# One of the seven products of an attention kernel's last V projection, moved from the projection into the third-last step

## The chip, the cores and the metric

The kernel runs on one core of one Trainium2 chip. The metric is the device time of one execution in microseconds, the median of several; less is better.

## The reference

`x` has 8 batches of 512 tokens with 512 features; there are 16 heads of 32. Of each batch:

```python
Q, K, V = heads(x @ Wq.T + bq), heads(x @ Wk.T + bk), heads(x @ Wv.T + bv)
cQ = Q + heads(cond @ Wq.T + bq)      # one condition token per batch
cK = K + heads(cond @ Wk.T + bk)
attn = softmax(cQ @ cK.T / sqrt(32))  # per head, 512 x 512
out = x + merge(attn @ V)
```

All inputs, outputs and the large matmuls are float32.

## The kernel before

**Steps.** The work is cut into T = 32 steps: step t is one batch b = t // 4 and one group g = t % 4 of four heads (128 columns of the output). The last batch, b = 7, is steps 28 to 31. Each step has four quarters (in the last steps called rows), one for each block of 128 keys. In quarter i of step t the program issues, in this order:

- `exponentials(t, i)`: four short matmuls (L560) that put the negated row maxima into four PSUM banks, four matmuls (L563) that add the scores, with the keys along the partitions, and four exponentials on ACT (L574) from PSUM to SBUF.
- `row_max(t + 1, i + 1)` (of step t + 2 in the last quarter): four score matmuls for the next step (L499), each into a bank of its own, and their maxima on DVE (L490 for one bank, L508 for two). Up to step 29 ACT then also runs `denominators` on them (L518, each followed by a read of its accumulator).
- one more piece of PE work: a part of the next batch's projections, or `weighted`, the exponentials times V (L579) with the sum of the denominators (L610).

The engines' orders are written out by hand (a manual schedule), so each engine issues its instructions in the order of the program, and semaphores are set where data or a bank demands it.

**Banks.** All eight PSUM banks are one tile. `banks(i)` is the i-th bank of the present line of the table `TURNS`: entries 0 to 3 go to the exponentials, 4 to 7 to the row maxima. The quarter's extra work reuses entries 0 to 3 after ACT has read them. `advance()` goes to the next line; in the last three steps `row(i)` sets it to `TURNS[8 + i]`:

```python
(4, 5, 6, 7, 0, 1, 2, 3),   # row 0
(6, 7, 0, 1, 2, 3, 4, 5),   # row 1
(0, 1, 2, 3, 4, 5, 6, 7),   # row 2
(2, 3, 4, 5, 6, 7, 0, 1),   # row 3
```

**Projections.** Q, K and V of a batch are made with Strassen's scheme in Winograd's form: seven products of half-size blocks (L403 for V, L406 for Q and K), each of two matmuls of 128 x 256 (two records each in the trace), for each half u = 0, 1. `first_products` does products 1, 6, one of the two matmuls of product 2, and 7; `other_products` does 4, 5, the rest of 2, and 3. So each call has seven matmuls. ACT copies product 1 to SBUF (L438) and DVE adds the others up: L444, L445 and L426 (in `plus`) after the first, L458, L459 and L426 after the others. In between `small()` calls `transpose_max` (L544 on PE, L550 on DVE), which prepares the next step's maxima.

V lies in `vs[b % 2]` as [128, 4, 512]: four blocks of 128 tokens and 512 features. `parts_of` names its parts for half u: c1 and c12 in the left 256 columns (heads of groups 0 and 1), c2 and c22 in the right 256 (groups 2 and 3). Product 7 goes only into the right half.

Batch 7's projections are made in steps 25 to 28: Q in the first quarter, K in the third, V in the fourth, by `project_pair`. Steps 25 and 27 call the `first` form, 26 and 28 the `other`. V's left half is first read in step 29, its right half in step 30 (`part_of(t, banks(0), [0])` with t = 30).

**The last three steps** (29, 30, 31) have no projections left. Their extra work is `part_of`: times V for single key blocks, copied out by ACT (L775, L769) and added by POOL (L770); `masked` and `spread_sums` for the denominators (POOL L600, PE L610). From step 30 on the program for DVE also adds exponentials up (L845, L847), and the end is a chain of DVE, PE and ACT.

Of the kernel before, what the change touches and what calls it, by code (L numbers as in the profile page):

```python
# [12 lines left out]
ALU = mybir.AluOpType  # L13
# [4 lines left out]
def kernel(  # L18
# [38 lines left out]
    nc = tc.nc  # L57
    P = 128
    B, S, D = x.shape
# [9 lines left out]
    HS = S // 2  # L69
# [41 lines left out]
    def banks(i, n=1):  # L111

        j = TURNS[turn[0]][i]
        if n == 1:
            return psum[:, j, :]
        k = TURNS[turn[0]][i + 1]
        return psum[:, j : k + 1 : k - j, :]
# [127 lines left out]
    for i in range(NS):  # L245
        r = slice(i * BL, (i + 1) * BL)
# [95 lines left out]
    def pair_of(t, n):  # L342

        if (n, t // 2) not in pairs:
            pairs[n, t // 2] = qkp.tile([P, 2, S], F32, tag=n, name=f"{n}T_{t // 2}")
        return pairs[n, t // 2]
# [30 lines left out]
    def block_of_w(n, i, u, kc):  # L377
        f = MADE_OF[i - 1][0]
        if n == "v":
            at = slice(0, HS) if f != "22" else slice(HS, D)  # L380
            if isinstance(f, int):
                return wc[n][:, f, kc, :]
        else:
            g = u * 2 + (f == "22")
            at = slice(g * P, (g + 1) * P)
            if isinstance(f, int):
                return wc[n][:, f, kc, u * P : (u + 1) * P]
        return wT[n][:, kc + 2 * (f != "11"), at]

    def block_of_x(b, i, kc, at):  # L390
        f = MADE_OF[i - 1][1]
        if isinstance(f, int):
            return xc[:, f, kc, at]
        off = HS * (f == "22")
        return xT[b][:, kc + 2 * (f != "11"), at.start + off : at.stop + off]

    def product(n, b, u, i, pt, kcs=(0, 1)):

        for kc in kcs:
            w = block_of_w(n, i, u, kc)  # L400
            if n == "v":
                xb = block_of_x(b, i, kc, slice(u * P, (u + 1) * P))
                nc.tensor.matmul(pt, xb, w, start=(kc == kcs[0]), stop=(kc == kcs[-1]))  # L403
            else:
                xb = block_of_x(b, i, kc, slice(0, HS))
                nc.tensor.matmul(pt, w, xb, start=(kc == kcs[0]), stop=(kc == kcs[-1]))  # L406

    def twice(a):
        return a.unsqueeze(1).broadcast_to([P, 2, HS])

    def halves(a):
        return a.rearrange("p (h s) -> p h s", h=2)


    def parts_of(n, b, u):

        if n == "v":
            v = vs[b % 2]
            return v[:, u::2, :HS], v[:, u + 2, :HS], v[:, u::2, HS:], v[:, u + 2, HS:]
        o = pair_of(b * G + u * 2, n)  # L420
        return halves(o[:, 0, :]), o[:, 0, HS:], halves(o[:, 1, :]), o[:, 1, HS:]
# [26 lines left out]
    def other_products(n, b, u, dens, small, at):  # L448
# [12 lines left out]
        if n != "v":  # L461
            for g in range(2):
                qkT[n, b * G + u * 2 + g] = pair_of(b * G + u * 2, n)[:, g, :]

    def project_pair(n, b, r, dens, small, at):

        if b >= B:
            dens()
            small()
        else:  # L470
            (first_products, other_products)[r % 2](n, b, r // 2, dens, small, at)


    nmax = {}
# [7 lines left out]
    def row_max(t, qc):  # L482
        if t >= T:
            return
        open_max(t)
        for j in range(HG):
            row_scores(t, qc, j, banks(HG + j))
        if t < T - 2 or t * NS + qc == T * NS - 1:
            for j in range(2):
                nc.vector.tensor_reduce(  # L490
                    nmax[t][:, qc, j : j + 1, 0], banks(HG + j), AX.X, ALU.max, negate=True
                )
        else:
            row_max_of(t, qc, 0, banks(HG, 2))
        row_max_of(t, qc, 1, banks(HG + 2, 2))
# [16 lines left out]
    def denominators(t, qc, prs=range(NP)):  # L512

        if t >= T - 2:
            return
        for j in [pr * 2 + i for pr in prs for i in range(2)]:
            dead = op.tile([P, S], F32, tag="dead", name=f"dead_{t}_{qc}_{j}")
            nc.scalar.activation(  # L518
                dead,
                banks(HG + j),  # L520
                AF.Exp,
                bias=nmax[t][:, qc, j, :],
                accum_out=sums[t][:, qc, j, :],
            )
# [14 lines left out]
    def transpose_max(t, bank, copy=nc.vector.tensor_copy):  # L539
        if t >= T:  # L540
            return
        pt = bank.bitcast(BF16)
        for qc in range(NS):
            nc.tensor.transpose(  # L544
                pt[:, qc * P : (qc + 1) * P],
                split[t % 2][:, qc, :, :].rearrange("p h e -> p (h e)"),
                identb,
            )
        maxT[t] = op.tile([P, S], BF16, tag="maxT", name=f"maxT_{t}")
        copy(maxT[t], pt[:, :S])  # L550
# [4 lines left out]
    def exponentials(t, kc, at=None):  # L555

        bank = [psum[:, i, :] for i in at] if at else [banks(i) for i in range(HG)]
        for j in range(HG):
            r = slice(j * HD, j * HD + 3)
            nc.tensor.matmul(bank[j], onesb[r, :], maxT[t][r, :], start=True, stop=False)  # L560
        for j in range(HG):
            r = slice(j * HD, (j + 1) * HD)
            nc.tensor.matmul(  # L563
                bank[j],
                qkT["k", t][r, kc * P : (kc + 1) * P],
                qkT["q", t][r, :],
                start=False,
                stop=True,
            )
        for pr in range(NP):  # L570
            e = ep.tile([P, 2, S], F32, tag="e", name=f"e_{t}_{kc}_{pr}")
            es[t, kc, pr] = e
            for i in range(2):
                nc.scalar.activation(e[:, i, :], bank[pr * 2 + i], AF.Exp)  # L574

    def times_v(t, kc, pt, chunks=range(NS)):
        b, g = divmod(t, G)
        for j in range(HG):
            nc.tensor.matmul(  # L579
                pt[j * HD : (j + 1) * HD, :],  # L580
                vs[b % 2][:, kc, (g * HG + j) * HD : (g * HG + j + 1) * HD],
                es[t, kc, j // 2][:, j % 2, :],
                start=(kc == chunks[0]),
                stop=(kc == chunks[-1]),
            )
# [11 lines left out]
    def masked(t):  # L597

        apart = op.tile([P, HG, NS, NS], F32, tag="apart", name=f"apart_{t}")
        nc.gpsimd.tensor_tensor(  # L600
            apart,
            sums[t].rearrange("p c h o -> p h c o").broadcast_to([P, HG, NS, NS]),
            which.unsqueeze(1).unsqueeze(1).broadcast_to([P, HG, NS, NS]),
            ALU.mult,
        )
        return apart

    def spread_sums(apart, pd):
        for h in range(HG):
            nc.tensor.matmul(  # L610
                pd[h * BL : (h + 1) * BL, :NB],
                modulo,
                apart[:, h].rearrange("p c a -> p (c a)"),
                start=True,
                stop=True,
            )
# [144 lines left out]
    def part_of(t, pt, of, between=None):  # L761

        for k, kc in enumerate(of):
            if k and between:
                between()
            times_v(t, kc, pt, of)
        if t in parts:
            p = op.tile([P, S], F32, tag="dead", name=f"part_{t}_{of[0]}")
            nc.scalar.copy(p, pt)  # L769
            nc.gpsimd.tensor_tensor(parts[t], parts[t], p, ALU.add)  # L770
        else:
            if not parts:
                parts["all"] = stage.tile([P, NC, D], F32, tag="w", name="parts")
            parts[t] = parts["all"][:, t % NC, :]
            nc.scalar.copy(parts[t], pt)  # L775

    def denominators_of(t, pd):

        den = op.tile([P, NB, 1], F32, tag="den", name=f"den_{t}")
        nc.scalar.copy(den, pd[:, :NB].unsqueeze(2))  # L780
        return den
# [6 lines left out]
    for t in range(T - 3):  # L788
        b, r = divmod(t, G)
# [4 lines left out]
        dens = lambda: denominators(t + 1, 1)  # L794
# [11 lines left out]
        dens = lambda: denominators(t + 1, 2)  # L806
# [13 lines left out]
        dens = lambda: denominators(t + 1, 3)  # L820
# [11 lines left out]
        dens = lambda: denominators(t + 2, 0)  # L832

        def small():
            transpose_max(t + 1, banks(2 if r % 2 else 1))
# [17 lines left out]
    def row(i):  # L853
        turn[0] = 8 + i
# [9 lines left out]
    exponentials(t, 1)  # L864
    row_max(t + 1, 2)
    part_of(t - 1, banks(0), [2])
    apart = masked(t - 1)
    row(2)
    exponentials(t, 2)
# [2 lines left out]
    part_of(t - 1, banks(0), [3])  # L872
    spread_sums(apart, banks(1))
    den = denominators_of(t - 1, banks(1))
    row(3)
    exponentials(t, 3)
    row_max(t + 2, 0)
# [69 lines left out]
    b, g = divmod(t, G)  # L947
# [48 lines left out]
```

## Time and profile before

| | us |
|---|---|
| median of 3 runs (732.04 to 732.4) | 732.4 |
| profiled execution, whole | 734.05 |
| its span, first to last instruction | 732.3 |
| PE busy with matmuls | 722.3 |
| ACT busy | 617.7 |
| DVE busy | 535.7 |
| POOL busy | 177.0 |

The granted clock of TensorE was 0.997 of full speed over the span. Engine shares are of the span; a busy PE includes pipelined matmuls that overlap. "L499" is line 499 of the kernel before. Where the text gives starts of single instructions to a hundredth of a microsecond, they are the trace's records, counted from the span's start. "x8" of a float32 matmul group means records: each float32 matmul leaves two.

### The profile page before, as it was taken

The page shows a single profiled execution, that of the slowest core. Times are in us where ns is not written, and L with a number is a line of the kernel's source. Part 1 is how long each engine was busy: PE and PEld are TensorE (multiplying, and loading weights), DVE is VectorE, ACT ScalarE, POOL GpSimd, SP SyncE. Part 2 cuts the span into 40 slices and gives each one's busy share as a digit, 9 for nine tenths or more (in the row PEclk, how much of TensorE's full clock was granted, in tenths as well). Part 3 has the DMA queues.
Part 4 walks back from the last instruction along what each step waited for, and adds up shares of the span by engine and source line. Part 5 has one row for each costly group of instructions (what it writes and reads, how often), then busy time and mean ns, then how long its engine had stood idle before and what let it go on. Part 6 is the DMA issues. An engine that isn't in the chain of part 4 may idle for free.

```text
span 732.3 us, 15085 instructions
## 1 busy us (share of the span) xinstructions
PE 722.3 (99%) x5396; PEld 401.8 (55%) x5396; DVE 535.7 (73%) x857; ACT 617.7 (84%) x1540; POOL 177.0 (24%) x276
## 2 busy tenths in 40 slices
PE   8999999999999999999999999999999999999996
PEld 5466555566555566555566555566555566555431
DVE  4698767777768777678676777677677777667676
ACT  2489988989898898898899898898898899898664
POOL 3622221122221122221122221122221122221351
PEclk9999999999999999999999999999999999999998
DMA  7734221222221222221222221222110111110121
GB/s 185 118 49 72 45 39 22 43 35 40 45 36 27 42 35 39 45 44 21 38 40 35 44 41 27 37 40 34 30 30 11 21 30 30 30 30 13 18 30 30
DMA packets 208111, 29.64 MB, mean 40 GB/s; under 512 B 205722, under 2 KB 206746, under 8 KB 208036
## 3 DMA queue, kind: packets, MB, share of 16 engines
q1 hardware_dynamic: 207184, 27.88, 23.7%
q8 instruction: 42, 0.69, 0.4%
q10 hardware_dynamic: 852, 0.81, 0.4%
q14 instruction: 33, 0.27, 0.1%
HBM read 20.27 MB, written 8.39 MB: 39 GB/s over the span
## 4 chain that ended last, share of the span: by engine, by line
PE 96%; DVE 2%; issue 1%; DMA 1%; SPq 0%; DVEq 0%
PE psum L406 26%; PE psum L499 16%; PE psum L579 15%; PE psum L563 14%; PE psum L403 14%; PE psum L560 6%; PE psum L350 2%; PE psum L544 1%; DMA x<-in_x_dram 1%; DVE acc L847 1%; PE psum L266 0%; DVE acc L845 0%; PE psum L657 0%; PE psum L589 0%; PE psum L610 0%
## 5 line engine op out<-in xcount | busy, mean ns | idle before, releaser
L518 ACT ACTIVATE dead<-psum,nmax 128x512 f32<-128x512 f32 x480 | 327.5, 702 | 5.3 <-DVE nmax L490 3.0
L574 ACT ACTIVATE e<-psum 128x512 f32<-128x512 f32 x512 | 264.3, 602 | 75.5 <-PE psum L563 75.4
L490 DVE TENSOR_REDUCE nmax<-psum 128x1 f32<-128x512 f32 x242 | 155.8, 685 | 143.3 <-PE psum L499 143.3
L508 DVE TENSOR_REDUCE nmax<-psum 128x2 f32<-128x1024 f32 x135 | 163.3, 1214 | 9.6 <-PE psum L499 8.3
L636 POOL TENSOR_TENSOR res<-res,recs 128x512 f32<-128x512 f32 x31 | 32.5, 1048 | 454.7 <-DVE res L635 454.7
L499 PE MATMUL psum<-kT,qT 32*128 32x512 f32 x1024 | 136.4, 601 | 0.0
L563 PE MATMUL psum<-qT,kT 32*128 32x512 f32 x1024 | 132.4, 588 | 0.0
L579 PE MATMUL psum<-e,v 128*32 128x512 f32 x1024 | 121.2, 596 | 0.0
L518 ACT ACTIVATION_READ_ACCUMULATOR dead<-psum,nmax 128x1 f32 x480 | 105.0, 219 | 0.0
L499 PEld LDWEIGHTS psum<-kT,qT 32*128 32x128 f32 x1024 | 58.1, 183 | 56.2 <-ACT dead L518 23.1
L579 PEld LDWEIGHTS psum<-e,v 128*32 128x32 f32 x1024 | 26.7, 110 | 65.8 <-issue 38.4
L563 PEld LDWEIGHTS psum<-qT,kT 32*128 32x128 f32 x1024 | 51.0, 185 | 2.2
L560 PE MATMUL psum<-maxT,onesb 3*128 3x512 bf16 x512 | 51.7, 384 | 0.5 <-DVE maxT L550 0.5
L403 PE MATMUL psum<-wc_v,xc 128*128 128x256 f32 x192 | 49.3, 379 | 0.0
L560 PEld LDWEIGHTS <-onesb 3*128 3x128 bf16 x512 | 13.4, 91 | 61.1 <-issue 51.7
L406 PE MATMUL psum<-xc,wc_q 128*128 128x256 f32 x180 | 46.2, 379 | 0.0
L406 PE MATMUL psum<-xc,wc_k 128*128 128x256 f32 x180 | 46.2, 379 | 0.0
L174 POOL TENSOR_TENSOR xr<-xr,bvs 128x512 f32<-128x512 f32 x31 | 39.4, 1270 | 17.6 <-DMA xr<-in_x_dram 17.6
L637 POOL TENSOR_TENSOR res<-res,xr 128x512 f32<-128x512 f32 x31 | 39.5, 1273 | 2.4
L403 PEld LDWEIGHTS psum<-wc_v,xc 128*128 128x128 f32 x192 | 36.5, 190 | 5.0
L403 PE MATMUL psum<-wT_v,xT 128*128 128x256 f32 x128 | 38.7, 405 | 0.0
L406 PEld LDWEIGHTS psum<-xc,wc_q 128*128 128x128 f32 x180 | 34.2, 190 | 4.7
(157 smaller groups left out, 771.5 us busy)
## 6 DMA issues: line engine op xcount, KB each, us to landing
xr<-in_x_dram SPq DMA_DIRECT2D x124, 64.0 KB, 2.4
out_dram<-res SPq DMA_DIRECT2D x124, 64.0 KB, 2.0
x<-in_x_dram SPq DMA_DIRECT2D x112, 64.0 KB, 2.4
w_q<-in_L_cond_Wq_dram SPq DMA_DIRECT2D x4, 256.0 KB, 4.9
w_v<-in_L_cond_Wv_dram SPq DMA_DIRECT2D x16, 64.0 KB, 2.5
w_k<-in_L_cond_Wk_dram SPq DMA_DIRECT2D x16, 48.0 KB, 2.4
x<-in_x_dram SPq DMA_DIRECT2D x2, 256.0 KB
x<-in_x_dram ACTq DMA_DIRECT2D x2, 256.0 KB, 4.4
```

What stands on the lines that cost most here:

```text
L174: nc.gpsimd.tensor_tensor(xr[t], xr[t], bias, ALU.add)
L403: nc.tensor.matmul(pt, xb, w, start=(kc == kcs[0]), stop=(kc == kcs[-1]))
L406: nc.tensor.matmul(pt, w, xb, start=(kc == kcs[0]), stop=(kc == kcs[-1]))
L490: nc.vector.tensor_reduce(nmax[t][:, qc, j : j + 1, 0], banks(HG + j), AX.X, ALU.max, negate=True)
L499: nc.tensor.matmul(pt, qkT["q", t][r, qc * P : (qc + 1) * P], qkT["k", t][r, :], start=True, stop=True,)
L508: nc.vector.tensor_reduce(nmax[t][:, qc, pr * 2 : pr * 2 + 2, 0], pt, AX.X, ALU.max, negate=True)
L518: nc.scalar.activation(dead, banks(HG + j), AF.Exp, bias=nmax[t][:, qc, j, :], accum_out=sums[t][:, qc, j, :],)
L560: nc.tensor.matmul(bank[j], onesb[r, :], maxT[t][r, :], start=True, stop=False)
L563: nc.tensor.matmul(bank[j], qkT["k", t][r, kc * P : (kc + 1) * P], qkT["q", t][r, :], start=False, stop=True,)
L574: nc.scalar.activation(e[:, i, :], bank[pr * 2 + i], AF.Exp)
L579: nc.tensor.matmul(pt[j * HD : (j + 1) * HD, :], vs[b % 2][:, kc, (g * HG + j) * HD : (g * HG + j + 1) * HD], es[t, kc, j // 2][:, j % 2, ...
L637: nc.gpsimd.tensor_tensor(y, y, xr.pop(t), ALU.add)
```

## The change

For V of the last batch, `project_pair` calls two new forms without product 7. The first does products 1, 6 and the whole of 2, the other 4, 5 and 3: six matmuls each instead of seven. DVE adds the parts up without product 7: still two additions after the first and three after the other, but c2 is added first, and c12 is updated twice after it. `add_m7(u, bank)` does product 7 later, two matmuls into a bank, and one addition of 128 x 2 x 256 on DVE into the right half of V. It is called in step 29: for u = 0 in row 1, after `part_of(t - 1, banks(0), [2])`, into `banks(1)` (bank 7); for u = 1 in row 2, after `denominators_of`, into `banks(2)` (bank 2). ACT, POOL and DMA instructions stay what they were.

```diff
+    def first_but_m7(n, b, u, dens, small, at):
+        one_, two_ = banks(0), banks(at)
+        c1, c12, c2, c22 = parts_of(n, b, u)
+        m1 = c2[:, 0, :]
+        product(n, b, u, 1, one_[:, :HS])
+        nc.scalar.copy(m1, one_[:, :HS])
+        dens()
+        product(n, b, u, 6, two_[:, :HS])
+        small()
+        product(n, b, u, 2, two_[:, HS:])
+        nc.vector.tensor_tensor(c12, two_[:, :HS], m1, ALU.add)
+        nc.vector.tensor_tensor(c1[:, 0, :], two_[:, HS:], m1, ALU.add)
+
+    def other_but_m7(n, b, u, dens, small, at):
+        dens()
+        one_, two_ = banks(at[0]), banks(at[1])
+        product(n, b, u, 4, one_[:, :HS])
+        product(n, b, u, 5, one_[:, HS:])
+        small()
+        product(n, b, u, 3, two_[:, :HS])
+        c1, c12, c2, c22 = parts_of(n, b, u)
+        nc.vector.tensor_tensor(c2, halves(one_), twice(c12), ALU.add)
+        nc.vector.tensor_tensor(c12, one_[:, HS:], c12, ALU.add)
+        nc.vector.tensor_tensor(c12, two_[:, :HS], c12, ALU.add)
+
+    def add_m7(u, pt):
+        c2 = parts_of("v", B - 1, u)[2]
+        product("v", B - 1, u, 7, pt[:, :HS])
+        nc.vector.tensor_tensor(c2, twice(pt[:, :HS]), c2, ALU.add)
+
     def project_pair(n, b, r, dens, small, at):
...
-            (first_products, other_products)[r % 2](n, b, r // 2, dens, small, at)
+            how = (first_products, other_products)
+            if n == "v" and b == B - 1:
+                how = (first_but_m7, other_but_m7)
+            how[r % 2](n, b, r // 2, dens, small, at)
...
     part_of(t - 1, banks(0), [2])
+    add_m7(0, banks(1))
     apart = masked(t - 1)
     row(2)
...
     den = denominators_of(t - 1, banks(1))
+    add_m7(1, banks(2))
     row(3)
     exponentials(t, 3)
```

## The prediction

> **What bounds the kernel now.** I read the page first (busy shares, then the chain that ended last), then the chain in order of time around the change, then the instructions of DVE and ACT beside it.
>
> ```profile
> span 732.3 us, 15085 instructions
> PE 722.3 (99%) x5396; PEld 401.8 (55%) x5396; DVE 535.7 (73%) x857; ACT 617.7 (84%) x1540; POOL 177.0 (24%) x276
> PE 96%; DVE 2%; issue 1%; DMA 1%; SPq 0%; DVEq 0%
> ```
>
> PE is the bound nearly everywhere, so 0.4 us of matmuls taken out of a PE-bound quarter can be worth 0.4 us, if ACT and DVE are ready that much sooner. The chain in order of time shows the quarter that loses a matmul (step 28, V) and the rows that gain the product (step 29):
>
> ```profile
> 678.67 1.92 PE psum L403 x8
> 680.59 0.22 PE psum L544 x4
> 680.81 1.35 PE psum L403 x6
> 682.16 0.33 PE psum L560 x4
> ...
> 689.11 0.72 PE psum L560 x4
> 689.82 0.86 PE psum L563 x8
> 690.68 1.02 PE psum L499 x8
> 691.70 0.99 PE psum L579 x8
> 692.70 0.05 PE psum L610 x7
> 692.75 0.66 PE psum L560 x4
> 693.40 0.86 PE psum L563 x8
> 694.26 1.02 PE psum L499 x8
> ```
>
> Columns: start, length, what. An L403 matmul is two records. L560 normally takes 0.33 and L499 0.86. In rows 2 and 3 of step 29 they take 0.72 and 1.02, then 0.66 and 1.02: 0.39 + 0.16 and 0.33 + 0.16 us of waiting, 1.04 in all, which extra matmuls could fill. DVE in the same rows:
>
> ```profile
> 688.15 2.36 DVE L508 TENSOR_REDUCE nmax<-psum 128x2 f32<-128x1024 f32 x2 [1.54 <-PE psum L499]
> 691.74 2.35 DVE L508 TENSOR_REDUCE nmax<-psum 128x2 f32<-128x1024 f32 x2 [1.23 <-PE psum L499]
> ```
>
> It reduces row 1's scores until 690.5 and row 2's until 694.1, and has 1.23 us free between. So its queue is far behind PE when PE enters row 3 at 692.75.
>
> **Part 1: a matmul less in each V quarter of steps 25 to 28.** Each quarter goes from 7 matmuls (14 records) to 6. Records of one run are 0.216 us apart, so PE needs 0.43 us less, four times: 1.72 us at most. DVE and ACT work there is the same in amount but does not start earlier, since it follows the scores at the quarter's head. So I ask when the next scores (L499 of the following row) find their banks free:
>
> ```profile
> 616.98 0.22 ACT L518 ACTIVATION_READ_ACCUMULATOR dead<-psum,nmax 128x1 f32 x1
> ...
> 638.98 0.20 ACT L518 ACTIVATION_READ_ACCUMULATOR dead<-psum,nmax 128x1 f32 x1
> ...
> 681.37 0.41 DVE L458 TENSOR_TENSOR v<-psum,v 128x256 f32<-128x256 f32 x1
> 681.70 0.68 DVE L459 TENSOR_TENSOR v<-psum,v 128x512 f32<-128x512 f32 x1
> 682.30 0.68 DVE L426 TENSOR_TENSOR v<-psum,v 128x512 f32<-128x512 f32 x1
> ```
>
> These are the last denominators of steps 25 and 26, and DVE's three additions of step 28. A release reaches PE about 0.05 us later (L508 ends at 690.51, L499 starts at 690.56).
> - Step 25: L499 started at 617.56 and could start at 617.13. The last denominator ends at 617.20 and holds one of its banks, so 617.25: 0.31 gained. Step 27 has the same spacing (661.35; denominator ends at 660.99): 0.31.
> - Step 28: L499 started at 683.18 and could at 682.75. The three additions are now in another order, 0.68, then 0.41, then 0.41, each waiting for the one before. From 681.37 they end at about 682.95 to 683.05, where L426 read its bank until 682.98 with nobody waiting. The fourth score uses that bank: start at about 683.03, 0.15 gained.
> - Step 26: L499 started at 639.40. Denominator until 639.18, additions from 637.60 until 639.2 to 639.3: about 0.10 gained.
>
> Sum: 0.87 us. The bounds are 0 and 1.72; I take the middle because each cover has a row. No DMA, SP or POOL instruction moves.
>
> **Part 2: the first product and addition, in row 1 of step 29.** Without a wait L560 would start at 689.04 (0.545 after the second half of L579, as at 685.45 to 686.00). The product's first record starts there, the second 0.32 later (656.76 to 657.08), two more at 0.216, then 0.31 to L560 (659.95 to 660.26). L560 starts at 690.10: four records cost 1.06 us, since the switches between tile shapes are paid once more. By then its banks are free and the 0.55 of waiting in row 2 is gone. Row 2 then runs clean: L563 at 690.33, L499 at 691.18, L579 at 692.15 (2.045 after L560, as 685.996 to 688.039) instead of 691.63. Row 2 is 0.51 us late. The first addition (0.68, by L459) lies in DVE's gap, 690.44 to 691.12, just before the fourth score needs bank 7 at 691.19. I price that new wait at nothing; if the addition is 0.2 us later, it is 0.2 us and a restart.
>
> **Part 3: the second product and addition, row 2.** This is where I expect the loss. The product goes to bank 2, which is the first bank of row 3's exponentials. In the changed program the first L560 of row 3 waits for DVE, where it waited for ACT. DVE is in order: the addition stands behind both reductions of row 2. L499's second half at 691.61, plus 0.63 (691.10 to 691.74), starts them at 692.24; the second starts 1.14 later, and the addition another 1.14 later, at 694.53. It ends at 695.2 and L560 starts at 695.26. The product itself is ready: after L610 (693.08) it starts at 693.2 to 693.4 and lands at 694.45 to 694.65, just about when DVE is free; so the addition may be up to 0.12 late. All of row 3 is queued behind that L560: L563, L499, ACT's exponentials and the next reductions. L579 of row 3 starts 2.045 later, at 697.3 to 697.4, instead of 695.22. That is 2.1 to 2.2 us late; with 0.1 for the restart (L499 took 1.14 instead of 1.03 after its wait at 690.56) I take 2.25. It contains Part 2's 0.51 and the used-up waits. After row 3 the chain runs PE, then DVE, without slack, until the end: nothing gives the time back. The POOL splits and the output DMAs shift with it.
>
> The nearest rows bound Part 3: if nobody waited for the addition, the rows would be 2.12 - 1.04 = 1.1 late; with a later addition and both restarts, 2.7.
>
> A page speaks on the addition's start: the Trainium skill, "VectorE: DVE Perf Modes", section "The DRAIN you can't avoid", says that the next op doesn't start until the pipe has emptied. The row differs: reductions recorded at 1.22 us start 1.14 apart. [...]
>
> The other is "TensorE: Matmul & The Clock Gate", section "Back-to-back issue gap": 262 cycles at 2.4 GHz, 0.109 us, for 256 columns. The rows have 0.216 between records. By the page a matmul would save 0.22 and the moved product would cost 0.44 plus the switches; the sum would come to about +1.7, because the addition's wait, not the product, sets row 3.
>
> **Sum.** 2.25 + 0.1 (small restarts in the V quarters, by 0.05 each where PE now waits a little, as for L499 at 677.56) - 0.87 = 1.5 us. The profiled execution took 734.05 us for a span of 732.3; the unprofiled median is 732.4. All of it lies inside the span, so 732.4 + 1.5 = 733.9. 0.2% is 1.46 us, about what a measurement can tell from no change; the forecast sits on that edge.
>
> **Rivals.**
> - **The waits in the tail pay for the product (not slower).** The 1.04 us of waiting in rows 2 and 3 and 1.72 saved against 2 x 1.06 spent gives -0.6, 731.8. It decides if the second addition ends before PE reaches row 3's L560, at 694.0 or so. Against it: row 2's reductions alone last until 694.6. It would need DVE 1.2 us sooner. 5%.
> - **The whole 0.43 four times is saved.** If the banks named in Part 1 are free sooner than I read, the loss is 2.25 - 1.72 = +0.5, 732.9. For it: ACT is idle 0.4 to 0.55 before the next exponentials; against it: scores, not exponentials, meet the last denominator. 12%.
> - **More waits.** The fourth score of row 2 waits for the first addition (0.25 with a restart) and the second product starts 0.4 late after L610, so the second addition does too: +2.1 to +2.6, 734.5 to 735.0. 20%.
> - That the product is not really moved is excluded by the order of the instructions: PE has 4 matmuls less in steps 25 to 28 and 4 more in step 29.
>
> **How the numbers follow.** The forecast (60%) spans +1.1 to +2.0, 733.5 to 734.4. Of it I count 37 of 100 as over 0.2% and 23 as within, since its middle lies just over the edge and unseen small waits add rather than take away. Slower: 37 + 20 = 0.57. Same: 23 + 12 + 5 = 0.40. Faster by over 0.2%: 0.03, for what I don't see. Range: +0.4 (whole saving) to +2.6 (more waits), 732.8 to 735.0.
>
> **What would show it.** In the changed profile: L403 x4 after L544 in the V quarters of steps 25 to 28, with L499 after them starting late behind ACT or DVE; row 2 of step 29 without its 0.55 of waiting; L560 of row 3 with over 1 us of waiting, released by DVE's addition. If that L560 runs in 0.33, Part 3 is wrong. If L499 after the V quarters starts a full 0.43 earlier, Part 1 is.

## The result, and the profile after

| | before | changed | ratio (95% interval) |
|---|---|---|---|
| median of 10 runs, us | 732.4 (732.0 to 732.74) | 734.15 (733.95 to 734.5) | 1.0024 (1.0015 to 1.0032) |

The change costs 1.75 us: 734.15 us, where 1.5 and 733.9 us were forecast. "L" and a number is a line of the kernel, "x4" a count of records.

The profile on record of the kernel before began late: its first x lands at 6.4 us, that of the changed kernel at 4.4, and by step 25 it lies 1.7 us behind (that step's V quarter starts at 613.04, in the changed kernel at 611.37). So both spans read 732.3 us. A second profile of the kernel before (told below) spans 730.9, and all differences of trace times from here on are against that one, called the reference. Its V quarter of step 25, with the scores (L499) behind it:

```profile
611.69 1.92 PE psum L403 x8
613.61 0.22 PE psum L544 x4
613.84 1.35 PE psum L403 x6
615.19 0.33 PE psum L560 x4
615.52 0.86 PE psum L563 x8
616.38 0.86 PE psum L499 x8
```

The page of the changed kernel shows PE as busy as before:

```profile
span 732.3 us, 15085 instructions
PE 723.5 (99%) x5396; PEld 403.2 (55%) x5396; DVE 536.2 (73%) x857; ACT 617.4 (84%) x1540; POOL 176.9 (24%) x276
```

The chain of the changed kernel in order of time (start, length, what), for the next scores behind the V quarters of steps 25 and 26, then the quarter of step 28 with what follows, then rows 1 to 3 of step 29. Lines of the code have moved: L594 is the old L560, L597 the old L563, L533 the old L499, L613 the old L579, L578 the old L544, L644 the old L610, L542 the old L508.

```profile
615.63 1.09 PE psum L533 x8
...
637.27 1.35 PE psum L533 x7
...
676.63 1.92 PE psum L403 x8
678.56 0.22 PE psum L578 x4
678.78 0.92 PE psum L403 x4
679.70 0.33 PE psum L594 x4
680.03 0.86 PE psum L597 x8
680.89 1.32 PE psum L533 x7
...
687.11 1.06 PE psum L403 x4
688.17 0.33 PE psum L594 x4
688.49 0.86 PE psum L597 x8
689.35 0.92 PE psum L533 x8
690.27 2.18 DVE nmax L542 x2
692.45 0.08 issue
692.53 0.69 DVE v L494
693.22 0.04 issue
693.26 0.40 PE psum L594 x4
693.66 0.86 PE psum L597 x8
694.52 0.86 PE psum L533 x8
695.38 0.99 PE psum L613 x8
```

Two things are to be seen. The quarter is shorter: L403 x4 for 0.92 where x6 took 1.35. But the scores behind it, 0.86 before, now take 1.09, 1.35 and 1.32: most of the gain comes back as waiting. And in row 2 the chain leaves PE: it runs through both reductions (L542) and the second addition (L494) before row 3's L594 starts at 693.26. PE and DVE there, instruction by instruction:

```profile
690.26 2.36 DVE L542 TENSOR_REDUCE nmax<-psum 128x2 f32<-128x1024 f32 x2 [1.15 <-PE psum L533]
692.53 0.68 DVE L494 TENSOR_TENSOR v<-psum,v 128x512 f32<-128x512 f32 x1
```

```profile
691.26 1.13 PE L403 MATMUL psum<-wc_v,xc 128*128 128x256 f32 x4
693.26 0.40 PE L594 MATMUL psum<-maxT,onesb 3*128 3x512 bf16 x4 [0.88 <-DVE v L494]
```

The product is finished at 692.39, the addition runs from 692.53 to 693.21, and PE sits idle for it (0.88 <-DVE v L494).

Where the time went, by the starts in the two chains (reference, changed):

| stretch | reference | changed | difference |
|---|---|---|---|
| V quarter of step 25 to the next L406 | 611.69 to 617.24 | 611.37 to 616.72 | -0.20 |
| step 26 | 633.53 to 639.07 | 633.01 to 638.62 | +0.07 |
| step 27 | 655.48 to 661.02 | 654.99 to 660.34 | -0.19 |
| step 28, to the next L579 | 677.32 to 682.86 | 676.63 to 682.21 | +0.04 |
| rows 1 and 2 of step 29 (L579 to row 2's) | 686.76 to 690.35 | 686.11 to 690.29 | +0.59 |
| row 3 (L579 of row 2 to row 3's) | 690.35 to 693.94 | 690.29 to 695.38 | +1.50 |

(Row 2's L613 is not in the chain of the changed kernel; its records start at 690.21, and the chain counts these groups 0.08 later.) The quarters give 0.28, with 0.05 between them 0.33 (71.17 us from the V quarter of step 25 to row 0 of step 29, now 70.84); the tail, rows 1 to 3 of step 29, costs 2.09. The difference, 1.76, is the 1.75 of the medians.

### The profile page after: what moved, and what is told of

Same layout as the page of the kernel before. It is cut to its first block, busy times and chain, and to the rows that moved or that the text cites. A ratio compares the mean times of both kernels' runs of the same rounds, so it can differ in the third digit from the quotient of the medians.

```text
span 732.3 us, 15085 instructions
## 1 busy us (share of the span) xinstructions
PE 723.5 (99%) x5396; PEld 403.2 (55%) x5396; DVE 536.2 (73%) x857; ACT 617.4 (84%) x1540; POOL 176.9 (24%) x276
## 4 chain that ended last, share of the span: by engine, by line
PE 96%; DVE 2%; issue 1%; DMA 0%; DVEq 0%
PE psum L406 26%; PE psum L533 16%; PE psum L613 15%; PE psum L597 14%; PE psum L403 14%; PE psum L594 6%; PE psum L350 2%; PE psum L578 1%; DVE acc L881 1%; DMA x<-in_x_dram 0%; DVE nmax L542 0%; PE psum L311 0%; DVE acc L879 0%; PE psum L266 0%; PE psum L691 0%
## 5 line engine op out<-in xcount | busy, mean ns | idle before, releaser
L542 DVE TENSOR_REDUCE nmax<-psum 128x2 f32<-128x1024 f32 x135 | 163.5, 1216 | 10.4 <-PE psum L533 10.4
L533 PE MATMUL psum<-kT,qT 32*128 32x512 f32 x1024 | 137.6, 601 | 0.0
L597 PE MATMUL psum<-qT,kT 32*128 32x512 f32 x1024 | 132.0, 587 | 0.0
L613 PE MATMUL psum<-e,v 128*32 128x512 f32 x1024 | 121.2, 597 | 0.0
L533 PEld LDWEIGHTS psum<-kT,qT 32*128 32x128 f32 x1024 | 58.9, 183 | 56.5 <-ACT dead L552 20.4
L613 PEld LDWEIGHTS psum<-e,v 128*32 128x32 f32 x1024 | 26.7, 110 | 65.8 <-issue 38.4
L594 PE MATMUL psum<-maxT,onesb 3*128 3x512 bf16 x512 | 51.0, 384 | 1.4 <-DVE v L494 0.9
L597 PEld LDWEIGHTS psum<-qT,kT 32*128 32x128 f32 x1024 | 51.0, 185 | 2.2
L403 PE MATMUL psum<-wc_v,xc 128*128 128x256 f32 x192 | 49.5, 380 | 0.0
L594 PEld LDWEIGHTS <-onesb 3*128 3x128 bf16 x512 | 13.2, 90 | 61.3 <-issue 51.9
L406 PE MATMUL psum<-xc,wc_q 128*128 128x256 f32 x180 | 46.2, 379 | 0.0
L406 PE MATMUL psum<-xc,wc_k 128*128 128x256 f32 x180 | 46.2, 379 | 0.0
L403 PEld LDWEIGHTS psum<-wc_v,xc 128*128 128x128 f32 x192 | 36.3, 190 | 5.7 <-ACT e L608 0.8
L403 PE MATMUL psum<-wT_v,xT 128*128 128x256 f32 x128 | 38.3, 404 | 0.0
L406 PEld LDWEIGHTS psum<-xc,wc_k 128*128 128x128 f32 x180 | 34.2, 190 | 4.7
```

Source lines behind the costliest of these rows:

```text
L533: nc.tensor.matmul(pt, qkT["q", t][r, qc * P : (qc + 1) * P], qkT["k", t][r, :], start=True, stop=True,)
L542: nc.vector.tensor_reduce(nmax[t][:, qc, pr * 2 : pr * 2 + 2, 0], pt, AX.X, ALU.max, negate=True)
L597: nc.tensor.matmul(bank[j], qkT["k", t][r, kc * P : (kc + 1) * P], qkT["q", t][r, :], start=False, stop=True,)
L613: nc.tensor.matmul(pt[j * HD : (j + 1) * HD, :], vs[b % 2][:, kc, (g * HG + j) * HD : (g * HG + j + 1) * HD], es[t, kc, j // 2][:, j % 2, ...
```

## The experiments

Each was timed beside the kernel before on the same chip; differences are of medians. The intervals reach about 0.09%, 0.7 us, to each side: they settle the big terms, and the traces the small ones.

**The kernel before again** (no edit).

> The kernel before, unchanged, for a second profile beside its first one. Time: no change, within 0.3 us. The profile of the record began 1.6 us later than that of the changed kernel (the first x lands at 6.4 us there and at 4.4 us here); if that is an accident of one execution, this span is about 730.6 us, and the steps up to the 24th lie where they lie in the changed kernel.

Measured: 732.43 against 732.4, ratio 0.9999 (0.9990 to 1.0008); span 730.9. The late start did not come again. In this trace step 25 lies 0.3 us later than in the changed kernel, not quite where it was expected; in the first profile it lies 1.7 us later.

**Part 1 alone: product 7 left out.**

```diff
-    add_m7(0, banks(1))
-    add_m7(1, banks(2))
```

> The changed kernel with product 7 of the last V left out altogether (neither made nor added), so that only the shorter V quarters remain. Theory: each shortened quarter meets the last denominator on ACT or the last addition on DVE, and the score group that waits for them loses 0.1 us more when it restarts. From the chain of the changed kernel the four quarters gain 0.19, -0.07, 0.19 and -0.04 us beside the profile before: 0.3 us faster than before in all. Rival one, the prediction as it stands: about 0.8 faster. Rival two, PE alone sets the quarters: 1.7 faster.

Measured: 732.14 against 732.43, ratio 0.9995 (0.9986 to 1.0004): 0.29 faster, within the noise but far from the 1.7 of PE alone; the time by itself doesn't exclude 0.8. Its trace does: from the V quarter of step 25 to row 0 of step 29 it takes 70.84 us (612.24 to 683.08), the reference 71.17 (611.69 to 682.86). So Part 1 is worth 0.33, not the 0.8 of the prediction.

**The two covers of Part 1 cut.**

```diff
+            w = BL if qc == 0 and j == 3 and 27 <= t <= 29 else S
             nc.scalar.activation(
-                dead,
-                banks(HG + j),
+                dead[:, :w],
+                banks(HG + j)[:, :w],
...
-        nc.vector.tensor_tensor(c12, two_[:, :HS], c12, ALU.add)
```

(on top of the kernel without product 7)

> As the one without product 7, and in addition the last denominators of the V quarter of steps 25 to 27 run over 32 keys instead of 512 and product 3 is not added, which takes away what I hold to be the limits of the shorter quarters. Theory: the scores now find their banks free, PE's 0.43 us comes out in all four quarters, 1.6 to 1.7 us faster than before. Rival: if PE's own sequence (switches between tile shapes) ate the gain, the time stays where the kernel without product 7 is, about 0.3 faster than before.

Measured: 730.71 against 732.43, ratio 0.9978 (0.9969 to 0.9987): 1.72 faster, the whole of 4 x 0.43. Its chain behind the V quarter of step 26:

```profile
635.26 0.92 PE psum L403 x4
636.18 0.33 PE psum L594 x4
636.51 0.86 PE psum L597 x8
637.37 0.86 PE psum L532 x8
638.23 3.22 PE psum L406 x14
```

The scores (L532 here) take 0.86 again instead of 1.35. So the quarters were held by ACT's last denominator and DVE's last addition, and by nothing in PE's own sequence. The two covers were cut together; which holds which step was not run apart, but is read from the records: in the changed kernel the last denominator of step 25 ends at 615.53 and the waiting score starts at 615.584; in step 28, which has no denominators, the last addition ends at 681.035 and the fourth score starts at 681.089; in step 26 both come, at 637.31 and 637.44, with scores at 637.364 and 637.494. The two rows of steps 25 and 28:

```profile
615.31 0.22 ACT L552 ACTIVATION_READ_ACCUMULATOR dead<-psum,nmax 128x1 f32 x1
680.61 0.42 DVE L489 TENSOR_TENSOR v<-psum,v 128x256 f32<-128x256 f32 x1
```

**The tail alone.** Full V projection, and products and additions in rows 1 and 2, into a part of V that is read no more.

```diff
-            if n == "v" and b == B - 1:
+            if False:
...
-        nc.vector.tensor_tensor(c2, twice(pt[:, :HS]), c2, ALU.add)
+        spare = parts_of("v", B - 2, u)[2]
+        nc.vector.tensor_tensor(spare, twice(pt[:, :HS]), c2, ALU.add)
```

> The kernel before with its full V projection, plus the two products and two additions in rows 1 and 2 of step 29 at their places, the additions going to a part of SBUF that nobody reads any more. So only the tail of the change. Theory: the second addition ends 2.09 us later than row 3 needed it, as in the changed kernel: 2.1 us slower than before. Rival (the waits of rows 2 and 3 pay for half of the products): 1.1 slower.

Measured: 734.42 against 732.43, ratio 1.0028 (1.0017 to 1.0040): 1.99 slower. In the trace L579 of row 1 to that of row 3 takes 9.27 us (686.51 to 695.78), in the reference 7.18 (686.76 to 693.94): 2.09. The two parts alone add up to the whole: 1.99 - 0.29 = 1.70 of 1.75.

**Another bank for the second product.**

```diff
-    spread_sums(apart, banks(1))
-    den = denominators_of(t - 1, banks(1))
-    add_m7(1, banks(2))
+    spread_sums(apart, banks(2))
+    den = denominators_of(t - 1, banks(2))
+    add_m7(1, banks(1))
```

> The changed kernel with two banks exchanged in row 2: the sum of the denominators goes to bank 2, product 7 of the second half to bank 1. Bank 2 is the first that row 3 needs, bank 1 the last (the fourth score, 1.1 us later). Theory: the addition of 0.68 us still ends at the same time, but nobody is late for it; row 3 starts 0.94 us sooner, and the time is 0.94 below the changed kernel, 0.8 slower than before. Rival: if the price of the tail is the product itself and its switches, or if the fourth score then waits as long, nothing changes: 1.75 slower than before.

Measured: 733.31 against 732.43, ratio 1.0013 (1.0004 to 1.0021): 0.88 slower. The same product and the same addition cost 0.9 us less in another bank than in the changed kernel; in the traces, L579 of row 1 to that of row 3 takes 8.35 us (686.22 to 694.57) instead of 9.27. Chain and DVE of rows 2 and 3:

```profile
691.47 1.06 PE psum L403 x4
692.53 0.33 PE psum L594 x4
692.86 0.86 PE psum L597 x8
693.72 0.86 PE psum L533 x8
694.57 0.99 PE psum L613 x8
```

```profile
692.64 0.69 DVE L494 TENSOR_TENSOR v<-psum,v 128x512 f32<-128x512 f32 x1
```

The addition ends at 693.33 (the rows lie 0.1 later here), after L594 has run; only the fourth score needs its bank, and L533 takes a clean 0.86. So of the 1.50 lost in row 3, 0.9 was the choice of the bank, with the place of the addition behind the reductions. The other 0.6 (690.39 to 694.57, 4.18 against 3.59) stays: the product's 1.06 less the 0.49 of waiting that it filled.

**Each half alone.** First half only (`r < 2` in the condition, no `add_m7(1, ...)`), and second half only (`r >= 2`, no `add_m7(0, ...)`):

> Only the product 7 of the first half moved (steps 25 and 26 shortened, product and addition in row 1 of step 29), the second half as before. Theory: row 2 starts 0.58 us late, since 0.55 us of waiting there goes and 1.06 us of PE comes; the quarters give 0.12 back: 0.4 to 0.5 slower than before. Rival (the product in the waits is free): 0.1 to 0.3 faster.

> Only the product 7 of the second half moved (steps 27 and 28 shortened, product and addition in row 2 of step 29), the first half as before. Theory: the addition behind both reductions holds row 3's first bank: 1.58 late, 0.15 given back by the quarters: 1.4 slower than before. Rival (the two halves cost alike): 0.9 slower.

Measured: 732.72 against 732.4, ratio 1.0004 (0.9995 to 1.0013), and 733.77 against 732.4, ratio 1.0019 (1.0010 to 1.0028): 0.32 and 1.37 slower, the first inside the noise; together 1.69 of the 1.75. In the traces the first half's row 1 to row 2 takes 4.18 us (686.43 to 690.61) against 3.59, so 0.59 more; the second half's row 1 to row 3 takes 8.75 (686.29 to 695.04) against 7.18, so 1.57 more. Second half alone:

```profile
692.19 0.69 DVE v L494
692.88 0.04 issue
692.92 0.40 PE psum L594 x4
```

The addition holds row 3 without any help from the first half.

**Towards a version that pays.** On top of the exchanged banks, product 1 is copied by DVE, where it had a gap, and the maxima of step 28 by ACT, which is idle there:

```diff
         product(n, b, u, 1, one_[:, :HS])
-        nc.scalar.copy(m1, one_[:, :HS])
         dens()
...
         small()
+        nc.vector.tensor_copy(m1, one_[:, :HS])
...
-            transpose_max(t + 1, banks(2 if r % 2 else 1))
+            copy = nc.scalar.copy if t == T - 4 else nc.vector.tensor_copy
+            transpose_max(t + 1, banks(2 if r % 2 else 1), copy)
```

> The changed kernel with the exchanged banks, and with two copies put where an engine is free: the copy of product 1 in the shortened V quarters goes from ACT to DVE (behind the copy of the maxima), so that the last denominator ends about 0.3 us sooner, and the copy of the maxima in step 28 goes from DVE to ACT, so that DVE's three additions start 0.33 sooner. Theory (ACT's denominators and DVE's additions limit the quarters): steps 25 and 27 give their full 0.43, step 28 about 0.3, step 26 stays at -0.07, the tail costs 1.17: 0.1 slower than before, 0.8 faster than with the exchanged banks alone. Rival (the longer queue on DVE takes back what ACT gives): 0.9 slower than before.

> The same, but only the second half moved (steps 27 and 28, product and addition in row 2); the first half as in the kernel before. Theory: 0.43 + 0.3 gained, and the product costs 1.06 less the 0.49 us of waiting in row 3: 0.57. So 0.15 faster than before, at the edge of what can be measured. Rival: 0.4 slower.

Measured: both halves 733.12 against 732.61, ratio 1.0007 (0.9998 to 1.0016): 0.51 slower, between theory and rival. Second half alone 732.59 against 732.61, ratio 0.9998 (0.9989 to 1.0007): no difference, and the interval takes in theory (0.15 faster) and rival (0.4 slower) alike. Its trace is on the theory's side: the V quarter of step 25 to L579 of row 3 takes 82.14 us (611.76 to 693.90), in the reference 82.25. In the trace with both halves moved the scores behind the V quarters take 0.90 (steps 25 and 27), 1.34 (step 26) and 0.99 (step 28), so the easing works where it was made. But in step 26's first quarter DVE's last Q addition (L429) now starts 0.4 us after the matmul it needs, and the next scores wait for it:

```profile
620.08 0.31 issue
620.39 0.76 DVE qT L429
621.15 0.04 issue
621.20 1.14 PE psum L533 x8
```

0.34 us of step 25's gain go there. What L429 waits for in that place the trace doesn't settle. No version beats the kernel before by more than a measurement can tell.

## Why the prediction was right, step by step

- **Part 3 holds, in mechanism and size.** 2.25 was forecast for the whole tail, 2.09 measured. Row 1's L579 starts at 686.11 here and at 688.11 in the first profile; shifted by these 2.0 us, the second addition was forecast at 692.53 and started at 692.53; L594 at 693.26, and it started at 693.264. Only the 0.1 for a restart of L594 didn't come: L597 follows it 0.215 later, as after a clean start.
- **Part 2 holds.** 0.51 forecast, 0.59 measured. The fourth score did wait for the first addition, but it cost only about 0.07 us (its first half lasts 657 ns beside 586), where the prediction had put nothing.
- **Part 1 is the term that was mis-sized.** Forecast 0.87 gained less 0.1 for restarts; measured 0.33 in all. The starts of the waiting scores came out as forecast in steps 25 and 27 (0.31 each, aligned to the reference), lower in 26 and 28 (0.03 and 0.05 for 0.10 and 0.15): between one addition of the chain and the next DVE lost up to 0.13 us (L488 ends at 680.48, L489 starts at 680.61), not 0.03. The larger miss is the restart: a score group that has waited takes 0.53 us from its last first half to its last second half and not 0.43, so about 0.1 in each of the four quarters, 0.4 in all, where 0.1 was put down for all. (In steps 25 and 27 DVE also has one addition less, so its work is not the same in amount as the prediction says; it is ACT that ends last there.)
- **The nearness of the sum is in part luck.** Part 1 came out 0.44 us worse than forecast (0.33 for 0.77), the tail 0.16 better. The two errors pull against each other and leave the 0.25 by which the sum was missed.
- **The rivals.** That the waits pay for the products falls with the tail alone (+1.99) and with the addition's end. That the whole 0.43 comes four times is right only with both covers cut. "More waits" had its first half in small (0.07), not its second: the product followed L610 (now L644) 0.11 later, not 0.4.

In the Trainium skill, "VectorE: DVE Perf Modes", section "The DRAIN you can't avoid", says that the next op does not start until the pipe is empty, but it goes on that an op which is not held starts earlier. The prediction read only the first half. Here the addition started 1.13 us after the second reduction, whose record lasts 1.21, so 0.08 before that record's end; the row fits the second half.

The prediction's other page estimate, +1.7 by the section "Back-to-back issue gap" of "TensorE: Matmul & The Clock Gate", left out a step: with the page's 0.109 us between records the first product too would be 0.42 shorter, and row 2's scores, the reductions and the second addition that much sooner. It should read about +1.3, still an estimate. The measurement decides against the page's figure for these float32 matmuls: in the changed kernel's first product the records start at 687.356, 687.572 and 687.788, 0.216 apart.

The page "TensorE: Matmul & The Clock Gate", section "The mechanism" of Part 3, says that matmuls are strictly first in, first out. Step 25 agrees: only the second score's bank was held (by the denominator), but the third and fourth, whose banks were free since 615.3, started at 615.590 and 615.597, right behind the second at 615.584.

## What to carry to other kernels

Work that is taken from a PE-bound stretch is worth only the way to the next late engine: ask for each bank that the following matmuls need who reads it last, and when; here that turned 1.72 us into 0.33. A product put into a waiting gap brings an instruction of another engine with it, and it is that engine's queue, and the bank it holds, that sets the price: choose the bank that is needed last, which alone was worth 0.9 us of 2.1. And a group of score matmuls that is held at all paid about 0.1 us more than the wait here, since its weights are loaded only after the release, as the next section shows.

## What was not expected of the hardware

The restart: a score matmul that is held shows 692 instead of 587 ns for its first half and 0.53 instead of 0.43 us to the second one, in rows 2 and 3 of the kernel before and behind all four V quarters of the changed one. After the shortest wait (row 2 of the changed kernel) it is 657 ns and 0.50 us. L594, a matmul with three rows, showed no such extra after 0.88 us of idle PE.

The trace shows where the extra lies. Each matmul has a load of its weights, with a row of its own (PEld, as many on the page as PE). Three rows of the changed kernel: from the load of row 2's fourth score on, from that of step 28's fourth score on (in both with loads of the second halves behind it), and the loads of row 3's scores, which nothing holds:

```profile
689.16 0.29 PEld L533 LDWEIGHTS psum<-kT,qT 32*128 32x128 f32 x5 [0.21 <-DVE v L494]
681.09 0.29 PEld L533 LDWEIGHTS psum<-kT,qT 32*128 32x128 f32 x2 [0.17 <-DVE v L489]
693.91 0.21 PEld L533 LDWEIGHTS psum<-kT,qT 32*128 32x128 f32 x4 [0.22 <-issue]
```

The clean loads start 0.43 us before their matmuls (693.913, 694.339). A held one starts at the release: 681.088 in step 28, with its matmul at 681.089; 689.162 in row 2, 0.053 after the first addition's end, with its matmul at 689.198. A load lasts 0.18 us, and in both cases the matmul's first half ends 0.512 us after it. So the wait holds back the load of the weights too, and most of what is then left of the load is added to the wait: 0.105 of 0.180 us in step 28, 0.070 of 0.145 in row 2. L594's first load had run at 692.32, long before its release, which fits. The ends of matmul records are modelled, but the second halves start later too. No run changed a load alone.
